# Four graph layers in one kernel: the two lookups of a slot placed side by side on TensorE

## The chip, the cores and the metric

The kernel runs on one core of a Trainium2 chip, in one launch. The metric is the device time of the launch in microseconds. The engines of the core are TensorE (PE, with its weight loads as PEld), VectorE (DVE), ScalarE (ACT), GpSimd (POOL) and SyncE (SP, which issues DMAs). [...]

## The reference

Sixteen graphs of 1024 nodes with 128 features pass through four layers; each adds its result to its input and normalizes the rows. Layer 0 is attention under an adjacency mask. Layer 2 is a sum over neighbours and a small network. Layer 3 first thins the adjacency row after row (each row's removals change later rows), then makes three convolutions. Layer 1 is the one that matters here:

```python
p = jnp.einsum('bnd,do->bno', x, W1 - W2)
q = jnp.einsum('bnd,do->bno', x, W2)
pre = p[:, :, None, :] + q[:, None, :, :] + b
h = jax.nn.relu(pre) * adj[..., None]
return jnp.max(h, axis=2)
```

For every node and feature it needs the maximum of `q` over the node's neighbours.

## The kernel before, in words

**The trick of layer 1.** The 1024 neighbours are cut into 86 groups of 12 (`NP`), each group into two of six. For six neighbours there are 64 subsets. For each of them a table holds the maximum of `q` over the subset (`tables_of`, lines 470 to 489, on DVE). Which subset a node has is found by a product of its adjacency with a matrix of plus and minus ones (`count`, line 814), turned into a one-hot row of 64 by ACT (line 815, tile `hot`). The lookup is then a product of table and one-hot (`look_up`, line 845) into a PSUM tile `pg`, and DVE keeps the running maximum in `best` (line 910; line 904 for a graph's first group).

**The slot.** One group of one graph is one slot; there are 16 x 86 = 1376 of them, written out by `slot(s, last)`. A slot has two halves, `h` 0 and 1, each for 512 of the 1024 nodes. The PE work of a half:

- a lookup of the half: four matmuls of 64 rows each, two with the table's high part and two with its low part, as the table is kept as two roundings; its `pg` is one of two buffers (tag "wide"), so it has to wait until DVE has read the lookup before the last;
- "pieces": a step or two of everything else (attention, the thinning of the adjacency, layer 2), handed out by `advance` and `dilate_on`;
- in odd slots, in half 0, `low_part(s + 1)` (line 834), which subtracts the rounded table from the exact one and needs ACT's `high` (line 829);
- the count of the same half two slots ahead (line 814), and behind it on ACT the `hot` of line 815;
- in even slots, in half 1, `table(s + 2)` (line 826), which transposes the table for two slots.

Counts and tables share two PSUM banks (tag "subset"). Their users take turns: in an even slot count 0, count 1, table; in the odd slot after it count 0, count 1. So the table takes the bank of the same slot's count 0, once ACT has made `hot` of it, and the second count of an odd slot takes the bank of the table before, once ACT has made `low` of it (line 836).

**What sets the order.** Around the slots stands a manual schedule for PE, ACT, DVE and POOL: their instructions keep the order in which the Python code issues them. Which pieces a half gets comes from a plan in units of slots: each stream asks with a cost and a delay, `room` limits what a half may take, and the thinning (`dilation`) asks to be continued at slot numbers (`due`). The plan knows no times, only slots. On SP and for DMAs the framework chooses the order.

**The thinning** runs beside the slots, 32 blocks of 32 rows. In each block POOL works through 31 rows one after the other (lines 669 to 679), starting when DVE has written `rest` (line 655). Its result goes out and in again by DMA (lines 686 and 689, tile `hit_p`), and DVE takes it up in line 703, at a place in its list that the plan fixed. POOL continues with line 707.

**After the slots** layer 3's convolutions follow (from line 942 on), which the change doesn't touch.

Of the kernel before, what the change touches and what calls it, by code (L numbers as in the profile page):

```python
# [29 lines left out]
F32 = mybir.dt.float32  # L30
# [10 lines left out]
P = 128  # L41
# [33 lines left out]
def tile_graph_layers(ctx: ExitStack, tc, a, out):  # L75
    nc = tc.nc
    x, adj, adjT = a["x"], a["adj"], a["adjT"]
    halves = (slice(0, 512), slice(512, 1024))
# [6 lines left out]
    psum = None  # L85
# [9 lines left out]
    psum = setup.enter_context(tc.tile_pool(name="psum0", bufs=2, space=PSUM))  # L95
# [146 lines left out]
    def layers_012():  # L242
# [3 lines left out]
        psum = psums.enter_context(tc.tile_pool(name="psumA", bufs=1, space=PSUM))  # L246
# [129 lines left out]
        def attend(b):  # L376
            for t in range(T):
                yield ask("PE", 0.01, after=("e", b, t))
                if t == 0:
                    y = w4.tile([P, T, D], F32, name="y0", tag="xT")  # L380
                e, total = exps.pop((b, t))
                eT = w4.tile([P, T, P], F32, name="eT")
                for h in range(2):
                    yield ask("PE", 0.44, take=True, same=(h == 0))
                    p = shared("pe")
                    for c in range(4):
                        nc.tensor.transpose(p[:, c * P:(c + 1) * P],  # L387
                                            e[:, (4 * h + c) * P:(4 * h + c + 1) * P], ident)
                    yield ask("A", 0.59, give=True, same=True)
                    nc.scalar.copy(eT[:, 4 * h:4 * h + 4, :].rearrange("p c i -> p (c i)"), p)  # L390
                happened["back", b, t] = now
                for h in range(4):
                    yield ask("PE", 0.45, take=(h == 0), same=(h > 0))
                    if h == 0:
                        pav = shared("pav")[:, :D]
                    for c in range(2 * h, 2 * h + 2):
                        nc.tensor.matmul(pav, eT[:, c, :], values[b][:, c, :], start=(c == 0), stop=(c == T - 1))  # L397
                yield ask("V", 0.4, give=True)
                share = small.tile([P, 1], F32, name="share")
                nc.vector.reciprocal(share, total)  # L400
                nc.vector.scalar_tensor_tensor(y[:, t, :], pav, share, X[b][:, t, :], op0=ALU.mult, op1=ALU.add)
            yield from norm(X[b], y)
            happened["X1", b] = now
# [66 lines left out]
        def tables_of(b):  # L470

            if b:
                yield ask("V", 0, urgent=True, after=("tables", b - 1))
            for g0 in range(0, NP, TG):
                n_g = 2 * min(TG, NP - g0)
                yield ask("V", 0.01, same=True, urgent=True, after=("q", b))
                made.append((b, g0))
                yield ask("V", 0.1, same=True, urgent=True, after=("used", *made[-3]) if len(made) > 2 else None)
                qg = qs[b].rearrange("o (g s) -> o g s", s=GS)
                subs[b, g0] = w2.tile([P, TG, P], F32, name="sub", bufs=2)  # L480
                sub = subs[b, g0].rearrange("o t (a s) -> o (t a) s", a=2)
                nc.vector.memset(sub[:, :n_g, 0:1], LOWEST)
                for k in range(GS):
                    n = 1 << k
                    yield ask("V", 0.06 + n * n_g / 960, same=(n < 8), urgent=True)
                    nc.vector.tensor_max(sub[:, :n_g, n:2 * n], sub[:, :n_g, 0:n],  # L486
                                         qg[:, 2 * g0:2 * g0 + n_g, k:k + 1].to_broadcast([P, n_g, n]))
                happened["sub", b, g0] = now
            happened["tables", b] = now
# [255 lines left out]
        def load_x(b):  # L745
            X[b] = apool.tile([P, T, D], F32, name="X", bufs=3)
            nc.sync.dma_start(out=X[b], in_=x[b].rearrange("(t p) d -> p t d", p=P))
# [5 lines left out]
        def load_columns(at):  # L753
            b, c = divmod(at, T + 1)
            if at > 1:
                before, k = divmod(at - 2, T + 1)
                rows = min(CH, N - k * CH)
                begin = len(nc.cur_bb.bb.instructions)
                nc.sync.dma_start(out=adj8[before][k * CH:k * CH + rows], in_=AT[at - 2][:rows])
                behind(nc.cur_bb.bb.instructions[begin - 1], begin)  # L760
            if b < B:
                rows = min(CH, N - c * CH)
                t = AT[at] = apool.tile([CH, N], F8, name="AT", bufs=4)
                if rows < CH:
                    nc.gpsimd.memset(t, 0.0)
                nc.gpsimd.dma_start(out=t[:rows], in_=adjT[b, c * CH:c * CH + rows])

        An, AT, subs, qs, ps, values, exps, bests, hots, tables = ({} for _ in range(10))
# [8 lines left out]
        def start(stream, first=False):  # L777
            pending[stream] = [next(stream, None), -9]
            streams.insert(0 if first else len(streams), stream)
# [59 lines left out]
        def look_up(s, h, pg):  # L839

            at = s % 2
            for k, part in enumerate(tables[s - at]):
                for a in range(2):
                    rows = slice(64 * a, 64 * a + 64)
                    nc.tensor.matmul(pg[:, a], part[rows, at * P:(at + 1) * P], hots[s][rows, halves[h]],  # L845
                                     start=(k == 0), stop=(k == 1))

        def merge(b, h):
            best, s = bests[b], halves[h]
            nc.vector.tensor_max(best[:, 0, s], best[:, 0, s], best[:, 1, s])  # L850
# [5 lines left out]
        def dilate_on():  # L856
            nonlocal due, wants_bank
            if due <= now and not (wants_bank and taken >= 2 and given.get(taken - 2, 1e9) > now):
                after, cost, wants_bank = next(dilate, (B * NP, 0, False))
                due += after  # L860
                room["V"] -= cost

        def slot(s, last):

            nonlocal now
            now = s
            b, g = divmod(s, NP)
            if s >= 0 and g == 0:
                bests[b] = bests[b - 1] if b else w4.tile([P, 2, N], F32, name="best")
                if b + 1 < B:  # L870
                    start(tables_of(b + 1), True)
                    load_x(b + 1)
                    start(attend(b + 1))
                    start(scores(b + 1))
            if s >= 0 and g % PC == 0:
                load_columns(b * (T + 1) + g // PC + 2)
            for h in range(2):
                now = s + 0.5 * h
                for e in ROOM:
                    room[e] = min(room[e] + ROOM[e] / 2, ROOM[e] / (2 if e in ("PE", "V") else 1))  # L880
                if s >= 0:
                    pg = psum.tile([P, 2, 512], F32, tag="wide", name="pg", bufs=2)
                    look_up(s, h, pg)
                early = s >= 0 and due < now
                if early:
                    dilate_on()
                advance(("PE",))
                advance(("A", "V", "Pool"))
                if s >= 0 and not early:
                    dilate_on()  # L890
                if h == 0 and s % 2 and s + 1 < last:
                    low_part(s + 1)
                if s + 2 < last:
                    count(s + 2, h)
                    if h and s % 2 == 0:
                        table(s + 2)
                if s >= 0:
                    own = bests[b][:, :, halves[h]]
                    if g == 0:
                        if b:  # L900
                            if h:
                                merge(b - 1, h)
                            total(b - 1, h)
                        nc.vector.tensor_copy(own, pg)
                        if b and h:
                            start(rest(b - 1))
                    else:
                        if g == NP - 1 and h:
                            merge(b, 0)
                        nc.vector.tensor_max(own, own, pg)  # L910
            if s >= 0:
                hots.pop(s)
# [19 lines left out]
        with tc.manual_schedule(engines={mybir.EngineType.PE, mybir.EngineType.Activation, mybir.EngineType.DVE,  # L932
# [43 lines left out]
            psum = ctx.enter_context(tc.tile_pool(name="psum", bufs=2, space=PSUM))  # L976
# [396 lines left out]
```

## Time and profile before

| what | value |
|---|---|
| time before, median of 3 runs | 6092.29 us (6090.22 to 6098.08) |
| time of the profiled execution | 6090.76 us |
| its span, first to last instruction | 6089.0 us |
| mean granted TensorE clock | 0.972 |
| busy over the span: PE, DVE, ACT, POOL | 5556.8, 4873.7, 3992.1, 3642.6 us |
| first lookup to last maximum | 139.8 to 4980.8 us, 4841 us |
| lookup matmuls (line 845), high and low | 5504 of 505 ns, 5504 of 400 ns |
| maxima (line 910) | 2720 of 1215 ns |

How to read it: a matmul's row gives the time from its issue to its modelled end, and matmuls overlap, so PE's cost of a step is read from start to start in the timeline and not from the durations. "PE" in a wait is the matmul, "PEld" the load of its weights. A wait "A <- B" is idle time of A's engine that ended when B was done; "issue" means that the profile shows no release. Waits that run beside other work are in the same list as waits that cost time.

### The profile page before, as it was taken

What the parts mean: (1) busy time and instruction counts of PE and PEld (TensorE: products, weight loads), DVE (VectorE), ACT (ScalarE), POOL (GpSimd) and SP (SyncE); (2) the same over time, 40 slices, a digit from 0 to 9 for tenths busy, and PEclk for the clock granted to TensorE, in tenths of its full rate; (3) what the DMA queues carried; (4) which work ended last, traced back from release to release, by engine and by line L of the source; (5) the groups of instructions that cost most, each with busy time, mean ns of one, the idle gap of its engine ahead of it and who ended that gap; (6) DMA issues with size and microseconds to landing.
All of it is one profiled execution on the core that took longest, in us unless ns stands there. A gap on an engine that the chain in (4) does not pass through costs nothing.

```text
span 6089.0 us, 93282 instructions
## 1 busy us (share of the span) xinstructions
PE 5556.8 (91%) x30144; PEld 3035.5 (50%) x30250; DVE 4873.7 (80%) x7484; ACT 3992.1 (66%) x7362; POOL 3642.6 (60%) x11879
## 2 busy tenths in 40 slices
PE   5989999999999999999999999999999878999998
PEld 4545454545454545454545454545444435555654
DVE  2888888889889888888888888888889865555455
ACT  3767777777677767677767676767666644444855
POOL 2676767677767767677777777777777641110114
PEclk8999999999999999999999999999999989999999
DMA  6121312121212121212121212121211025554645
GB/s 41 12 35 24 41 26 39 26 41 27 39 26 40 26 38 27 38 27 39 28 38 27 39 26 39 26 38 27 38 27 30 13 54 141 142 143 135 217 164 194
DMA packets 496976, 334.28 MB, mean 55 GB/s; under 512 B 303338, under 2 KB 448228, under 8 KB 492388
## 3 DMA queue, kind: packets, MB, share of 16 engines
q1 hardware_dynamic: 405504, 260.29, 14.6%
q0 software_dynamic: 89008, 67.42, 13.0%
q8 instruction: 237, 3.88, 0.3%
q14 instruction: 255, 2.09, 0.1%
q10 hardware_dynamic: 1972, 0.59, 0.1%
HBM read 362.38 MB, written 133.96 MB: 82 GB/s over the span
## 4 chain that ended last, share of the span: by engine, by line
PE 33%; DVE 11%; ACT 4%; issue 2%; POOL 1%; DMA 1%; SPq 0%; DVEq 0%; ACTq 0%; POOLq 0%
PE pg L845 8%; DVE best L910 5%; PE pagg L1073 5%; PE pm L814 3%; PE po L1103 2%; PE pa L439 1%; PE po L1097 1%; PE pav L397 1%; PE pp L300 1%; ACT hot L815 1%; DVE sub L486 1%; PE prank L599 1%; PE pdeg L1028 1%; DVE near L1016 1%; PE pe L387 1%
## 5 line engine op out<-in xcount | busy, mean ns | idle before, releaser
L910 DVE TENSOR_TENSOR best<-best,pg 128x1024 f32<-128x1024 f32 x2720 | 3260.8, 1215 | 481.2 <-PE pg L845 470.4
L815 ACT ACTIVATE hot<-pm,one_less 128x512 fp32r<-128x512 f32 x2752 | 1889.9, 690 | 728.7 <-PE pm L814 722.6
L845 PE MATMUL pg<-hot,high 64*128 64x512 f32 x5504 | 1400.3, 505 | 204.5 <-DVE best L910 174.6
L845 PE MATMUL pg<-hot,low 64*128 64x512 f32 x5504 | 1109.9, 400 | 0.0
L814 PE MATMUL pm<-AT,lit 120*128 120x512 fp8e4 x2752 | 1079.4, 392 | 4.5 <-ACT low L836 3.5
L845 PEld LDWEIGHTS pg<-hot,high 64*128 64x128 f32 x5504 | 521.2, 186 | 956.1 <-DVE best L910 455.6
L669 POOL TENSOR_SCALAR sc<-low_counts,half_mask,rest 16x1 f32<-16x1 f32 x992 | 361.0, 364 | 395.8 <-DVE rest L655 285.0
L845 PEld LDWEIGHTS pg<-hot,low 64*128 64x128 f32 x5504 | 534.5, 191 | 0.0
L814 PEld LDWEIGHTS <-lit 120*128 120x128 fp8e4 x2752 | 269.1, 98 | 385.5 <-issue 309.3
L674 POOL TENSOR_SCALAR sc<-sc 16x1 f32<-16x1 f32 x992 | 396.4, 400 | 104.9
L836 ACT CAST low<-pt 128x256 fp32r<-128x256 f32 x688 | 256.5, 373 | 254.0 <-PE pt L834 252.8
L671 POOL TENSOR_SCALAR sc<-sc 16x1 f32<-16x1 f32 x992 | 329.1, 332 | 107.4
L1118 POOL TENSOR_TENSOR length<-length,mhalf 128x8 f32<-128x8 f32 x48 | 78.9, 1645 | 486.2 <-DVE length L1117 486.2
L676 POOL TENSOR_SCALAR hit<-V,sc 16x31 bf16<-16x31 bf16 (+30 forms) x992 | 364.5, 367 | 0.0
L677 POOL TENSOR_SCALAR last_rank<-V,sc 16x31 f32<-16x31 bf16 (+30 forms) x992 | 346.9, 350 | 0.0
L834 PE MATMUL pt<-high,less 128*128 128x256 f32 x688 | 277.0, 403 | 67.4 <-ACT high L829 61.5
L486 DVE TENSOR_TENSOR sub<-sub,q 128x24 f32<-128x24 f32 (+11 forms) x768 | 306.8, 401 | 24.7 <-ACT q L304 10.5
L826 PE MATMUL pt<-ident,sub 128*128 128x128 f32 x1376 | 277.0, 283 | 53.2 <-ACT hot L815 51.1
L397 PE MATMUL pav<-v,eT 128*128 128x128 f32 x2048 | 301.5, 292 | 2.0 <-ACT eT L390 2.0
L397 PEld LDWEIGHTS pav<-v,eT 128*128 128x128 f32 x2048 | 255.5, 196 | 73.3 <-issue 55.6
L670 POOL TENSOR_SCALAR sc<-sc 16x1 f32<-16x1 f32 x992 | 239.9, 242 | 86.6
L349 PE MATMUL psc<-kT,qT 128*128 128x256 f32 x1024 | 273.9, 385 | 9.7 <-issue 9.7
(270 smaller groups left out, 9666.2 us busy)
## 6 DMA issues: line engine op xcount, KB each, us to landing
removed<-gone SPq DMA_DIRECT2D x128, 256.0 KB
An<-in_adj_dram POOLq DMA_DIRECT2D x16, 1024.0 KB, 15.0
E<-in_adj_dram POOLq DMA_DIRECT2D x128, 128.0 KB, 6.5
gone_all<-removed POOLq DMA_DIRECT2D x64, 256.0 KB, 10.5
near<-adj SPq DMA_DIRECT2D x16, 1024.0 KB
kept<-near SPq DMA_DIRECT2D x16, 1024.0 KB
share<-share SPq DMA_DIRECT2D x32, 512.0 KB
hidden<-r SPq DMA_DIRECT2D x32, 512.0 KB
```

The costliest lines, as they stand in the source:

```text
L397: nc.tensor.matmul(pav, eT[:, c, :], values[b][:, c, :], start=(c == 0), stop=(c == T - 1))
L486: nc.vector.tensor_max(sub[:, :n_g, n:2 * n], sub[:, :n_g, 0:n], qg[:, 2 * g0:2 * g0 + n_g, k:k + 1].to_broadcast([P, n_g, n]))
L669: gp.tensor_scalar(half, mine, half_mask[:, m], rest[:, n:n + 1], op0=ALU.mult, op1=ALU.add)
L671: gp.tensor_scalar(sf, half, 5.5, sf, op0=ALU.is_gt, op1=ALU.mult)
L674: gp.tensor_scalar(to, at, sf, none, op0=ALU.subtract, op1=ALU.subtract)
L676: gp.tensor_scalar(hit[:, n, n + 1:], V[:, n, n + 1:], at, None, op0=ALU.is_equal)
L677: gp.tensor_scalar(last[:, n + 1:], V[:, n, n + 1:], to, None, op0=ALU.is_le)
L814: nc.tensor.matmul(pm, lit[:, r, :], AT[b * (T + 1) + c][:, halves[h]], start=True, stop=True)
L815: nc.scalar.activation(hots[s][:, halves[h]], pm, AF.Relu, bias=one_less)
L845: nc.tensor.matmul(pg[:, a], part[rows, at * P:(at + 1) * P], hots[s][rows, halves[h]], start=(k == 0), stop=(k == 1))
L910: nc.vector.tensor_max(own, own, pg)
L1073: nc.tensor.matmul(pa[:, s], piece[:, t, :], m[c][:, s], start=(i == 0), stop=(i == 15))
```

## The change

Before, each half began with its own lookup. After, both lookups stand at the beginning of the slot, into the two `pg` buffers, and the pieces and the counts of both halves come behind them. DVE's maxima stay where they were, each at the end of its half. The whole diff:

```diff
@@ -878,9 +878,10 @@
                 now = s + 0.5 * h
                 for e in ROOM:
                     room[e] = min(room[e] + ROOM[e] / 2, ROOM[e] / (2 if e in ("PE", "V") else 1))
-                if s >= 0:
-                    pg = psum.tile([P, 2, 512], F32, tag="wide", name="pg", bufs=2)
-                    look_up(s, h, pg)
+                if s >= 0 and h == 0:
+                    pgs = [psum.tile([P, 2, 512], F32, tag="wide", name="pg", bufs=2) for _ in range(2)]
+                    for i in range(2):
+                        look_up(s, i, pgs[i])
                 early = s >= 0 and due < now
                 if early:
                     dilate_on()
@@ -895,7 +896,7 @@
                     if h and s % 2 == 0:
                         table(s + 2)
                 if s >= 0:
-                    own = bests[b][:, :, halves[h]]
+                    own, pg = bests[b][:, :, halves[h]], pgs[h]
                     if g == 0:
                         if b:
                             if h:
```

The number of instructions of PE, DVE, ACT and POOL is the same. The lists of DVE, ACT and POOL are the same in order too. On PE the second lookup of each slot moves ahead of the first half's pieces and count. On SP a few DMAs change places with their neighbours.

## The prediction

> **What bounds the kernel now.** I read the page's busy times first, then the groups of instructions, then the waits within the stretch of the slots (139.8 to 4980.8 us), then the timeline of PE and ACT in one slot.
>
> ```profile
> PE 5556.8 (91%) x30144; PEld 3035.5 (50%) x30250; DVE 4873.7 (80%) x7484; ACT 3992.1 (66%) x7362; POOL 3642.6 (60%) x11879
> ...
> L910 DVE TENSOR_TENSOR best<-best,pg 128x1024 f32<-128x1024 f32 x2720 | 3260.8, 1215 | 481.2 <-PE pg L845 470.4
> L815 ACT ACTIVATE hot<-pm,one_less 128x512 fp32r<-128x512 f32 x2752 | 1889.9, 690 | 728.7 <-PE pm L814 722.6
> L845 PE MATMUL pg<-hot,high 64*128 64x512 f32 x5504 | 1400.3, 505 | 204.5 <-DVE best L910 174.6
> ```
>
> PE and DVE wait for each other: DVE stood 470 us for lookups, PE 204.5 us for maxima. The slots take 4841 us for 1376, 3.518 us each. DVE is busy for 4259.4 us of that stretch (3.10 us a slot), and PE less its waits for DVE takes 3.518 - 204.5/1376 = 3.37 us. So PE is the longer lap, and it is not all work:
>
> ```profile
> DVE best L910 <- PE pg L845: 470.4, 839, 8.8
> PEld pg L845 <- DVE best L910: 455.6, 978, 12.1
> PEld pg L845 <- issue: 378.2, 1395, 1.0
> PEld L814 <- issue: 309.3, 819, 0.7
> POOL num L707 <- DVE counts L530: 289.6, 31, 21.6
> POOL sc L669 <- DVE rest L655: 285.0, 30, 15.5
> ```
>
> The two "issue" rows (total, times, longest) are weight loads that no semaphore held: those ahead of a lookup and those of a count. They stand where PE goes from 128 (or 120) rows to 64 and back. The timeline of an even slot without pieces on PE shows them as starts that lie 0.32 us apart:
>
> ```profile
> 2003.85 0.39 PE L814 MATMUL pm<-AT,lit 120*128 120x512 fp8e4 x1
> 2004.17 0.50 PE L845 MATMUL pg<-hot,high 64*128 64x512 f32 x2
> 2004.51 0.40 PE L845 MATMUL pg<-hot,low 64*128 64x512 f32 x2
> 2004.84 0.39 PE L814 MATMUL pm<-AT,lit 120*128 120x512 fp8e4 x1
> 2005.37 0.44 PE L826 MATMUL pt<-ident,sub 128*128 128x128 f32 x2
> ```
>
> and ACT in the same slot:
>
> ```profile
> 2003.88 0.87 ACT L282 ACTIVATE X<-y,ln_mv 128x128 f32<-128x128 f32 x2
> 2004.65 0.67 ACT L815 ACTIVATE hot<-pm,one_less 128x512 fp32r<-128x512 f32 x1
> ```
>
> Here the table (L826, 2005.37) starts 0.05 us after `hot` of the first count is done (2004.65 + 0.67): its bank came free just then. The reader is to see that the lookup at 2004.17 fills the time in which ACT makes that `hot`.
>
> [...] a count followed by a lookup lasts 0.32 us from start to start[...]. [...] The trace shows PE lookups waiting, 314 times, and nothing passing them.
>
> **The change, part by part.** Durations are those of the profiled execution, 6090.8 us with 1.8 us outside its span; the median is 1.5 us above it.
>
> *Switches (gain).* One of two visits to 64-row mode a slot goes. From start to start over all slots: lookup low to anything else 0.325, within a stream 0.216[...]; high to low 0.333 against 0.216, so 0.12 for the exposed first weights; a count before a lookup 0.32 against 0.216, 0.10; and the first load behind the second lookup is no longer exposed, 0.01 for fp8 or bf16 to 0.10 for f32, 0.035 in the mix. Sum 0.366 us a slot, x 1376 = 503 us of PE. All of it lies on PE's own lap.
>
> *Low part behind ACT (gain).* L834 waits for `high` (60.8 us of PE) and L826 for `hot` (51.1 us). I remove both rows, 112 us or 0.08 a slot; what L826 waits in the new order comes next.
>
> *The table behind the count (cost).* In an even slot the second lookup leaves the place between count 0 and the table. Read from each of the 688 even slots: from count 0 to the end of its `hot` 1.32 us in the median (1.12 to 1.76), ACT's queue included. PE has to fill that with two counts (0.43) and the second half's pieces, which 37% of these slots don't have. The mean wait is 0.65 us per even slot, 448 us. In the slot above it is 5.37 - 3.85 - 0.43 = 1.09. From below: take the room that the trace shows today between `hot` and table (some of it made by PE's waits for DVE) and shorten it by the 0.76 us that the lookup and its switches took: 317 us.
>
> *The second count behind low (cost).* In odd slots it takes the bank that ACT's `low` (L836) frees, 0.90 us after the low part's matmul. With the lookup gone, 0.43 us and the pieces lie between: 0.31 us per odd slot, 211 us; from today's room 160 us. Together 659 us (477 from below), 0.48 (0.35) a slot. PE's lap is then 3.37 - 0.37 - 0.08 + 0.48 = 3.40, or 3.27 with the lower waits: no gain, or a tenth of a microsecond. In slots with pieces PE gets faster, in bare ones slower.
>
> *The wait for DVE (cost).* The second lookup now starts 0.55 us after the first and needs the slot's last maximum before, which DVE reaches only at the end of that slot. From a second lookup that is not held: the first maximum starts 0.23 us later (a lookup's result reaches DVE 0.775 after its start), 1.135 for it (two of them take 2.35), the second half's other DVE work V (0 in a quarter of slots, 0.34 median, 1.0 at 90%), 1.20 and a 0.05 handover: 2.61 + V before the next second lookup can start. Slot by slot against PE's lap (2.3 to 4.5 us), PE is short of that in many slots: 0.20 us mean with the long lap, 0.27 with the short one. Behind the waiting lookup stand both halves' pieces, both counts and the table, and ACT and POOL behind those. Before, a lookup needed a maximum two lookups back with pieces between, and its fresh result was 2.0 us away against a lap of 3.3. So 3.60 or 3.54 a slot. Of today's 0.149 a slot of waits for DVE's backlog some remains: none to all; I take a tenth.
>
> *Moved past nothing.* DVE, ACT and POOL keep their order, so their queues cost nothing by themselves; the few SP transfers that change places have tens of microseconds of plan around them.
>
> *Sum.* (3.60 + 3.54)/2 + 0.015 = 3.585 us a slot, 0.067 more, x 1376 = +92 us: 6183 for the profiled execution, **6184 us** against the median. The bounds are 3.27 with no new DVE wait and 3.60 + 0.149.
>
> **The rivals.**
>
> *Faster: the ACT waits fall into DVE's.* If the waits for `hot` and `low` are paid in time that PE would stand for DVE anyway, DVE is the lap. Adding up, slot by slot, the longer of PE's work and DVE's work gives 3.51 for the kernel before (measured 3.518), which speaks for it; with 0.366 less PE work and no ACT waits it gives 3.37, -200 us. The thinning takes part back. POOL's 31 rows take 120.5 us a block, the DMA back about 4.5 more, and DVE comes for it 129.9 us after `rest`: only some 5 us of slack a block, and DVE already stood 10.5 us for it at 409 us. With slots 4% shorter 109 us are won there and 27 in the rest of the block: -136, **5956 us**. It decides if ACT is done within PE's own next 0.43 us plus pieces; L826's start on the heels of `hot` speaks against it. A half success (lower waits and half the DVE wait, 3.27 + 0.27/2 = 3.405, with the same cap about -100; with some backlog -50) lies near 6040.
>
> *No change.* Switches saved equal the waits gained and the DVE wait is one that exists today: **6092 us**.
>
> *Much slower.* All the backlog comes on top, as PE has no lead left: 3.60 + 0.149 = 3.75, +318, **6410 us**. Against it: the `hot`s are two slots ahead, and DVE is never without a lookup for longer than one handover when PE is the one that waits.
>
> That the change doesn't do what it says can be left out: the instruction list of the changed kernel has the two lookups side by side, each with its own wait for a maximum.
>
> **How the numbers follow.** Moderately slower 0.61 (own range 6105 to 6310), much slower 0.07, no change 0.08, faster 0.24 (0.11 of it below 6000). About 0.2% (12 us) is what can be told from no change here. So faster 0.24, same 0.08, slower 0.68; the range 6000 to 6310 leaves 0.11 below and 0.07 above.
>
> **What would show it.** The loads "issue" of L845 and L814 fall by half or more, high's mean stays near 505 for first lookups and drops to about 390 for second ones. L826's wait for `hot` rises from 51 to over 250 us, a wait of L814 for `low` appears (today 3.3 us), PE's wait for L910 grows above 175 us. POOL's waits for L655 and L707 grow with the slot. It is wrong if these ACT waits stay under 150 us, or if DVE's idle time for lookups falls below 300 us; then the switches were worth what they look like.

## The result, and the profile after

| | before | after |
|---|---|---|
| median of 4 runs | 6091.26 us (6088.10 to 6098.08) | 6195.36 us (6183.61 to 6205.61) |
| profiled execution, span | 6090.76, 6089.0 us | 6205.61, 6203.9 us |
| mean granted TensorE clock | 0.972 | 0.965 |
| first lookup to last maximum, per slot | 3.524 us | 3.606 us |
| everything else | 1240 us | 1243 us |

The stretch of the slots is counted here from the start of the first lookup (133.0 us in before) to the end of the last maximum, 4849 us before and 4961 after; the 4841 us given for before above run from the start of the first maximum (139.8) to that of the last.

After is slower: ratio 1.0169 (1.0148 to 1.0190), 104 us. Of the 115 us between the two profiled spans 112 lie in the slots. From the page of after, the lines that answer to those of before (the maxima's line is now L911):

```profile
PE 5426.3 (87%) x30132; PEld 3090.5 (50%) x30250; DVE 4853.2 (78%) x7484; ACT 3935.6 (63%) x7362; POOL 3619.0 (58%) x11879
...
L911 DVE TENSOR_TENSOR best<-best,pg 128x1024 f32<-128x1024 f32 x2720 | 3240.7, 1214 | 494.4 <-PE pg L845 485.3
L815 ACT ACTIVATE hot<-pm,one_less 128x512 fp32r<-128x512 f32 x2752 | 1856.6, 690 | 602.4 <-PE pm L814 591.5
L845 PE MATMUL pg<-hot,high 64*128 64x512 f32 x5504 | 1325.7, 477 | 254.8 <-DVE best L911 224.0
L814 PE MATMUL pm<-AT,lit 120*128 120x512 fp8e4 x2752 | 1043.0, 394 | 91.0 <-ACT low L836 84.5
...
L826 PE MATMUL pt<-ident,sub 128*128 128x128 f32 x1376 | 295.6, 297 | 219.3 <-ACT hot L815 213.3
```

The page of before has for the last two:

```profile
L814 PE MATMUL pm<-AT,lit 120*128 120x512 fp8e4 x2752 | 1079.4, 392 | 4.5 <-ACT low L836 3.5
...
L826 PE MATMUL pt<-ident,sub 128*128 128x128 f32 x1376 | 277.0, 283 | 53.2 <-ACT hot L815 51.1
```

PE is busy 130 us less and stands longer: within the slots it is without a matmul for 630 us, against 382 before. From the waits of after between 139.8 and 5095 us, the stretch of its slots (total, times, longest):

```profile
DVE best L911 <- PE pg L845: 485.3, 558, 5.0
...
POOL num L707 <- DVE counts L530: 369.4, 31, 25.6
...
PEld pg L845 <- issue: 235.7, 829, 3.3
PE pg L845 <- DVE best L911: 224.0, 396, 3.4
PE pt L826 <- ACT hot L815: 213.3, 355, 6.7
...
PEld L814 <- issue: 105.4, 279, 0.7
PE pm L814 <- ACT low L836: 84.3, 283, 1.4
```

Against before: the loads "issue" fell (378.2 to 235.7, 309.3 to 105.4), the table's wait for `hot` rose from 51.1 to 213.3, the count's wait for `low` from 3.3 to 84.3. The timeline shows how, on PE in an even slot of after and at the head of the next:

```profile
2041.96 0.40 PE L590 MATMUL pturn<-ident_b,E 128*128 128x128 bf16 x4
2042.19 0.60 PE L814 MATMUL pm<-AT,lit 120*128 120x512 fp8e4 x2
2043.68 0.44 PE L826 MATMUL pt<-ident,sub 128*128 128x128 f32 x2 [0.89 <-ACT hot L815]
2044.04 0.50 PE L845 MATMUL pg<-hot,high 64*128 64x512 f32 x2
2044.38 0.40 PE L845 MATMUL pg<-hot,low 64*128 64x512 f32 x2
2045.26 0.50 PE L845 MATMUL pg<-hot,high 64*128 64x512 f32 x2 [0.48 <-DVE best L911]
```

on ACT:

```profile
2042.45 0.59 ACT L591 CAST ET<-pturn 128x512 bf16<-128x512 f32 x1 [1.46 <-PE pturn L590]
2042.93 1.27 ACT L815 ACTIVATE hot<-pm,one_less 128x512 fp32r<-128x512 f32 x2
```

and on DVE:

```profile
2041.99 1.21 DVE L911 TENSOR_TENSOR best<-best,pg 128x1024 f32<-128x1024 f32 x1
2043.12 0.95 DVE L486 TENSOR_TENSOR sub<-sub,q 128x768 f32<-128x768 f32 x1
2043.99 1.21 DVE L911 TENSOR_TENSOR best<-best,pg 128x1024 f32<-128x1024 f32 x1
```

Two waits. The two counts now follow each other at once. So the table at 2043.68 starts as soon as the first `hot` is done, which ACT began only after `ET` and ended at 2042.93 + 0.69 = 2043.62. And the second lookup, due at about 2044.61, starts at 2045.26, 0.06 after the maximum that frees its buffer (2043.99 + 1.21 = 2045.20); the step `sub` of 0.95 us stands on DVE between the slot's two maxima.

**The accounting used below.** Bracketed idle times count from a matmul's modelled end. So I took, from the trace, the distances from start to start on PE between first lookup and last maximum. For each pair of neighbouring kinds the fast end (12th percentile) counts as work, the rest as a wait of the later matmul; at the half clock, which the trace records, up to as much again is put down to the clock (in after the matmuls of L349 start 0.215 us apart at full clock and 0.427 at half, in the median). In us of the slot stretch ("lookups" includes the longer distance from a lookup's `high` to its `low` behind a hold, over 0.33 us against 0.23):

| kernel | median, us | ratio to before (95%) | work | half clock | lookups | table | count | low part |
|---|---|---|---|---|---|---|---|---|
| before | 6091.26 | | 4146 | 87 | 245 | 74 | 23 | 92 |
| after | 6195.36 | 1.0169 (1.0148–1.0190) | 3745 | 125 | 411 | 319 | 171 | 18 |
| lookups parted by pieces | 6217.3 | 1.0188 (1.0173–1.0203) | 4061 | 93 | 237 | 292 | 119 | 14 |
| lookups mid-slot | 6252.11 | 1.0247 (1.0232–1.0262) | 4018 | 136 | 375 | 51 | 168 | – |
| maxima together | 6096.14 | 0.9994 (0.9983–1.0005) | 3761 | 91 | 284 | 325 | 180 | 29 |
| mid-slot, maxima together | 6129.65 | 1.0046 (1.0030–1.0061) | 4002 | 141 | 330 | 56 | 161 | – |
| counts first | 6394.88 | 1.0491 (1.0468–1.0514) | 3856 | 199 | 596 | 147 | 89 | 63 |
| counts first, maxima together | 6183.65 | 1.0145 (1.0125–1.0165) | 3853 | 164 | 364 | 141 | 101 | 94 |
| before, counts first | 6255.97 | 1.0261 (1.0240–1.0283) | 4230 | 143 | 255 | 4 | 4 | 214 |
| before, odd slots side by side | 6186.3 | 1.0146 (1.0125–1.0168) | 4049 | 157 | 367 | 84 | 78 | 9 |

The rows stand beside before's runs on the same chip, with medians of 6091.26 to 6100.05 us. After against before: work -401, clock +38, lookups +166, table +245, count +148, low part -74, the rest -10: +112, the difference of the two stretches (4961 - 4849).

The accounting has a blind spot: a wait that comes back with almost the same length in most cases of a pair is taken for work. The fast end of such a pair is then longer than that of the same pair in other kernels, and this shows three cases. In the two mid-slot kernels a count behind a table in 271 slots (0.825 us from start to start; in after a lookup follows a table after 0.200) hides some 169 us of waiting. With odd slots side by side, a count behind a count in 272 slots (0.616 against 0.220) hides 108 us. In the relieved kernels of before's order further down, a low part behind a lookup in 271 slots (0.54 and 0.55 against 0.32) hides 58 and 62 us.

### The profile page after: what moved, and what is told of

It reads as the page before. It is cut to its first block, busy times and chain, and to the rows that moved or that the text cites. A ratio compares the mean times of both kernels' runs of the same rounds, so it can differ in the third digit from the quotient of the medians.

```text
span 6203.9 us, 93371 instructions
## 1 busy us (share of the span) xinstructions
PE 5426.3 (87%) x30132; PEld 3090.5 (50%) x30250; DVE 4853.2 (78%) x7484; ACT 3935.6 (63%) x7362; POOL 3619.0 (58%) x11879
## 4 chain that ended last, share of the span: by engine, by line
PE 29%; DVE 12%; ACT 5%; issue 3%; POOL 2%; DMA 1%; SPq 0%; DVEq 0%; ACTq 0%; POOLq 0%
PE pg L845 6%; DVE best L911 6%; PE pagg L1074 5%; PE pm L814 2%; PE po L1104 2%; ACT hot L815 2%; PE pav L397 1%; PE po L1098 1%; PE pa L439 1%; DVE sub L486 1%; PE pt L826 1%; PE pdeg L1029 1%; DVE near L1017 1%; PE pp L300 1%; PE prank L599 1%
## 5 line engine op out<-in xcount | busy, mean ns | idle before, releaser
L911 DVE TENSOR_TENSOR best<-best,pg 128x1024 f32<-128x1024 f32 x2720 | 3240.7, 1214 | 494.4 <-PE pg L845 485.3
L815 ACT ACTIVATE hot<-pm,one_less 128x512 fp32r<-128x512 f32 x2752 | 1856.6, 690 | 602.4 <-PE pm L814 591.5
L845 PE MATMUL pg<-hot,high 64*128 64x512 f32 x5504 | 1325.7, 477 | 254.8 <-DVE best L911 224.0
L814 PE MATMUL pm<-AT,lit 120*128 120x512 fp8e4 x2752 | 1043.0, 394 | 91.0 <-ACT low L836 84.5
L845 PE MATMUL pg<-hot,low 64*128 64x512 f32 x5504 | 1119.3, 401 | 0.0
L845 PEld LDWEIGHTS pg<-hot,high 64*128 64x128 f32 x5504 | 530.0, 188 | 1094.1 <-DVE best L911 570.4
L669 POOL TENSOR_SCALAR sc<-low_counts,half_mask,rest 16x1 f32<-16x1 f32 x992 | 357.1, 360 | 400.9 <-DVE rest L655 299.6
L845 PEld LDWEIGHTS pg<-hot,low 64*128 64x128 f32 x5504 | 540.8, 191 | 30.4
L826 PE MATMUL pt<-ident,sub 128*128 128x128 f32 x1376 | 295.6, 297 | 219.3 <-ACT hot L815 213.3
L674 POOL TENSOR_SCALAR sc<-sc 16x1 f32<-16x1 f32 x992 | 394.7, 398 | 105.1
L826 PEld LDWEIGHTS pt<-ident,sub 128*128 128x128 f32 x1376 | 154.9, 143 | 487.9 <-ACT hot L815 465.3
L671 POOL TENSOR_SCALAR sc<-sc 16x1 f32<-16x1 f32 x992 | 318.5, 321 | 107.7
L814 PEld LDWEIGHTS <-lit 120*128 120x128 fp8e4 x2752 | 236.8, 100 | 189.6 <-issue 105.4
L834 PE MATMUL pt<-high,less 128*128 128x256 f32 x688 | 281.7, 409 | 13.3 <-ACT high L829 13.0
L670 POOL TENSOR_SCALAR sc<-sc 16x1 f32<-16x1 f32 x992 | 239.5, 241 | 86.5
```

The lines of the kernel that those rows point to most:

```text
L669: gp.tensor_scalar(half, mine, half_mask[:, m], rest[:, n:n + 1], op0=ALU.mult, op1=ALU.add)
L671: gp.tensor_scalar(sf, half, 5.5, sf, op0=ALU.is_gt, op1=ALU.mult)
L674: gp.tensor_scalar(to, at, sf, none, op0=ALU.subtract, op1=ALU.subtract)
L814: nc.tensor.matmul(pm, lit[:, r, :], AT[b * (T + 1) + c][:, halves[h]], start=True, stop=True)
L815: nc.scalar.activation(hots[s][:, halves[h]], pm, AF.Relu, bias=one_less)
L826: nc.tensor.matmul(pt[:, k * P:(k + 1) * P], subs[b, g0][:, g - g0 + k, :], ident, is_transpose=True, start=(k == 0), stop=(k == 1))
```

## The experiments

The theory: switches are really saved, and the saving is paid back to ACT (table and second count, whose bank comes free late) and to DVE (second lookup). The rivals: the saving is smaller than it looks, or one of the two payments is all of it.

**Lookups parted by pieces.** From after, the second lookup goes behind the first half's pieces: the switches are back, ACT's neighbours stay close.

```diff
                 if s >= 0 and h == 0:
                     pgs = [psum.tile([P, 2, 512], F32, tag="wide", name="pg", bufs=2) for _ in range(2)]
-                    for i in range(2):
-                        look_up(s, i, pgs[i])
+                    look_up(s, 0, pgs[0])
...
                     dilate_on()
+                if s >= 0 and h == 0:
+                    look_up(s, 1, pgs[1])
                 if h == 0 and s % 2 and s + 1 < last:
                     low_part(s + 1)
```

> The changed kernel with the second lookup put behind the first half's pieces and still ahead of its count. Where a half has pieces the second visit to 64-row mode is back, so little of the switch gain is left, and the second lookup has pieces between it and the first. The count and the table stay as close to each other as in the change, so PE has to wait for ACT. Theory (ACT waits of table and second count plus the wait for DVE): the ACT waits alone, some 0.38 us a slot, are paid with little gained: 6190 to 6330 us. Rival 1 (only the second lookup's wait for DVE costs): that wait is mostly gone, 5950 to 6110 us. Rival 2 (the saved switches are no time at all): as the change, about 6195 us.

Measured 6217.3 us, in the range of the theory; "as the change", rival 2's forecast, lies in that range too, so this time alone doesn't tell the two apart. Rival 1's forecast was missed. Work is up by 316 us against after, lookups wait as little as in before (237), and yet the kernel is as slow as after: table and count still wait 411 us, against before's 97. With only 85 us of work saved against before, the waits for ACT alone (table, count and low part 425 us against 189) are enough for a loss of 117 us.

**Lookups mid-slot.** From after, both lookups go between the first half's count and the second half's pieces, so that they fill the time of ACT's `hot`.

```diff
                 if s + 2 < last:
                     count(s + 2, h)
                     if h and s % 2 == 0:
                         table(s + 2)
+                if s >= 0 and h == 0:
+                    pgs = [psum.tile([P, 2, 512], F32, tag="wide", name="pg", bufs=2) for _ in range(2)]
+                    for i in range(2):
+                        look_up(s, i, pgs[i])
+                if h == 0 and s % 2 and s + 1 < last:
+                    low_part(s + 1)
```

(the same lines are taken out above.)

> The changed kernel with both lookups in the middle of the slot, between the first half's count and the second half's pieces (the low part behind them). Still one visit to 64-row mode, and the lookups fill the time between count 0 and the table. Theory: L826's wait for ACT goes (213 us of idle PE in the change), L814's wait for low stays near 84 us, part of the gain returns as waits for the maxima; 3.49 us a slot, 5990 to 6110 us. Rival 1 (only the wait for DVE costs): as the change, 6175 to 6215 us. Rival 2 (the saved switches are no time): not below the kernel before, 6090 us or more.

Measured 6252.11 us: the theory missed by over 140. The rows of its page for maxima, counts and tables:

```profile
L911 DVE TENSOR_TENSOR best<-best,pg 128x1024 f32<-128x1024 f32 x2720 | 3244.6, 1215 | 705.8 <-PE pg L845 699.1
...
L814 PE MATMUL pm<-AT,lit 120*128 120x512 fp8e4 x2752 | 1066.0, 393 | 245.0 <-ACT hot L815 205.5
...
L826 PE MATMUL pt<-ident,sub 128*128 128x128 f32 x1376 | 273.6, 280 | 38.2 <-ACT hot L815 37.7
```

The table's wait went (213.3 to 37.7), as expected; the count now waits 205.5 us for `hot`. In the new order an odd slot's first count comes right behind a table, and the bank it takes is that of the even slot's second count, just issued. In 271 slots without pieces this wait is so regular (0.625 us) that the accounting has it as work; with it the count waits some 340 us. Five tiles rotate through two banks, and the one gap that two lookups make is in front of one tile only. I moved the wait to another neighbour, and expected it to go.

**Maxima together.** From after, both maxima stand at the end of the first half on DVE; PE's order is after's.

```diff
-                if s >= 0:
-                    own, pg = bests[b][:, :, halves[h]], pgs[h]
+                for i in range(2 if s >= 0 and h == 0 else 0):
+                    own, pg = bests[b][:, :, halves[i]], pgs[i]
...
-                        if b and h:
-                            start(rest(b - 1))
...
+                if h and s >= NP and g == 0:
+                    start(rest(b - 1))
```

> The changed kernel with both maxima of a slot following each other on DVE at the end of the first half, so that the second half's other DVE work no longer lies between a lookup and the maximum that the next second lookup waits for. Only DVE's order differs. Theory: the second lookup's wait for DVE shrinks by up to 0.15 us a slot, PE's idle time for L911 falls from 224 to under 120 us, the ACT waits stay: 6000 to 6120 us. Rival 1 (the ACT waits alone cost, and the wait for DVE follows from them): within 25 us of the change, 6170 to 6220 us.

Measured 6096.14 us over 12 runs, ratio 0.9994 (0.9983 to 1.0005): the whole loss is gone. From its page:

```profile
L909 DVE TENSOR_TENSOR best<-best,pg 128x1024 f32<-128x1024 f32 x2720 | 3189.3, 1215 | 451.4 <-PE pg L845 445.0
...
L845 PE MATMUL pg<-hot,high 64*128 64x512 f32 x5504 | 1298.0, 468 | 167.0 <-DVE best L909 146.1
...
L826 PE MATMUL pt<-ident,sub 128*128 128x128 f32 x1376 | 296.9, 298 | 226.1 <-ACT hot L815 221.6
```

The wait for maxima falls from 224.0 to 146.1 (under 120 was expected); the table's 221.6 doesn't move. With the second maximum ahead of the second half's DVE pieces its buffer is free earlier. In the accounting lookups lose 127 us of waiting and the clock 34. What remains against before is work saved (-385) and waits for ACT gained (table, count, low part: 534 against 189): that leaves 40 us, which the lookups' 39 more take.

**Mid-slot with maxima together.** Both edits, the maxima at the end of the second half.

> Lookups in the middle of the slot, and both maxima at the end of its second half on DVE, behind the other work of both halves. Theory: both new waits are mostly gone and the one saved visit to 64-row mode remains; DVE's work (3.1 us a slot) and POOL's chain of rows set the end: 5880 to 5990 us, and DVE waits for hit_p (L703) in more than ten of the 32 blocks. Rival 2 (the saved switches are no time): 6060 to 6110 us. Rival 1 as in the run with the maxima together: near 6050 us.

Measured 6129.65 us, above the range: the count's wait is as in the mid-slot kernel (161, and the same 169 us hidden in the work). DVE waited for `hit_p` in 2 blocks, where over ten were expected. The order on DVE is worth 122 us here.

**Counts first.** From after, the low part and the counts go ahead of the pieces, which are then to fill the time of `hot`; an odd slot's second count stays behind them.

```diff
+                if h == 0:
+                    if s % 2 and s + 1 < last:
+                        low_part(s + 1)
+                if s + 2 < last and not (h and s % 2):
+                    count(s + 2, h)
                 early = s >= 0 and due < now
...
-                if h == 0 and s % 2 and s + 1 < last:
-                    low_part(s + 1)
-                if s + 2 < last:
-                    count(s + 2, h)
-                    if h and s % 2 == 0:
+                if s + 2 < last and h:
+                    if s % 2:
+                        count(s + 2, h)
+                    else:
                         table(s + 2)
```

> The changed kernel with the counts and the low part put ahead of the half's pieces (only the second count of an odd slot stays behind its pieces), so that pieces lie between count 0 and the table and between the low part and the count that takes its bank. DVE's order is that of the change. Theory (ACT waits and the wait for DVE both cost): PE's idle time for hot at L826 and for low at L814, 298 us together in the change, falls under 90 us; a part comes back as waits for maxima; 5990 to 6080 us. Rival 1 (only the second lookup's wait for DVE costs, ACT waits lie beside it): 6175 to 6215 us as the change.

Measured 6394.88 us, the slowest of these kernels and over 300 us above the range. Its waits over the whole span:

```profile
ACT hot L815 <- PE pm L814: 846.3, 940, 4.0
...
PE pg L845 <- DVE best L915: 362.1, 509, 9.6
...
PE pe L387 <- ACT e L359: 95.6, 58, 2.7
PE pt L826 <- ACT hot L815: 91.4, 188, 0.6
```

The table's wait fell from 213.3 to 91.4, which was the point (with `low`'s 33.8 it is 125, where under 90 was expected). What made it slower I read like this, without a run that shows it: ACT's `hot` now stands in its list ahead of its pieces. When a held second lookup holds the count behind it, ACT stands at `hot` (846.3 us against 591.5 in after), its pieces start late, PE waits for those (95.6 against 29.1 in after), and DVE's steps behind them are late too, and with them the next maximum (362.1 against 224.0). That ACT stands at `hot` is no loss by itself: in before it did so for 722.6 us. I had looked at PE's order alone.

**Counts first with maxima together**, the edit of above on this kernel.

> As the run with the counts ahead of the pieces, and both maxima of a slot together at the end of its first half on DVE. Theory: both new waits are reduced, the saved switches stay: PE's lap near 3.1 us, DVE's work and POOL's chain near 3.1 to 3.4 us: 5900 to 5990 us. Rival 1: as the run with the maxima together alone, 6080 to 6110 us. Rival 2 (the saved switches are no time): not under the run that has the lookups apart and the counts ahead.

Measured 6183.65 us: 211 us better than without, but far above the range.

**Before, with counts first**: the same move in the kernel before.

> The kernel before with nothing changed but the counts and the low part put ahead of the half's pieces: lookups apart, two visits to 64-row mode a slot. It has only the 112 us of ACT waits of the kernel before to lose. Theory: 6030 to 6090 us, and the run with lookups together, counts ahead and maxima together is at least 60 us faster than this one, as it saves 0.366 us of switches a slot. Rival 2 (the saved switches are no time): the two within 30 us of each other, or this one faster.

Measured 6255.97 us, 160 us slower than before, so counts first is bad by itself: work +84, low part +122 (PE's wait of L834 for ACT's `high` is 177.4 us, against 60.8 in before), clock +56, against 89 less for table and count. The side-by-side kernel with the same counts and with its maxima together is faster than this one by 72 us (over 60 was expected), but without the moved maxima it is slower by 139. So the gain is that of both moves together, and what the maxima's order is worth with the lookups apart wasn't run.

**Banks.** In the whole kernel the lookups hold four PSUM banks (a bank here is a buffer of 128x512 f32), counts and tables two, everything else two; I ran no version of it with more for counts and tables. The four kernels below make room: as their expectation says, they leave out one of the two groups of a lookup with its maximum, and 15 of POOL's 31 row steps in each block. In before's trace the matmuls of the two groups start 0.003 us apart, so PE's distances were to stay without the second; its work by the accounting did (4212 to 4216 us in before's order against 4146, 3749 to 3752 in after's against 3745). DVE (busy 53 to 57% of the span) and POOL (34 to 37%) are then far from limiting. Two have before's order, two after's; one of each has four banks. The lines of the edit that matter here, four banks first:

```diff
-            pm = psum.tile([P, 512], F32, tag="subset", name="pm", bufs=2)
+            pm = psum.tile([P, 512], F32, tag="subset", name="pm", bufs=4)
...
-            pt = psum.tile([P, 512], F32, tag="subset", name="pt", bufs=2)[:, :2 * P]
+            pt = psum.tile([P, 512], F32, tag="subset", name="pt", bufs=4)[:, :2 * P]
...
-                for a in range(2):
+                for a in range(1):
                     rows = slice(64 * a, 64 * a + 64)
```

> The kernel before with DVE and POOL relieved, so that PE and ACT set the slot: it leaves out the second group of six in each lookup and maximum [...], and all but 16 of the 31 row steps of each block on POOL; the PSUM tile of a lookup is then one bank. Two banks for counts and tables, as before. Theory: PE's lap of before without waits for DVE, 3.2 to 3.37 us a slot: 5640 to 5880 us.

> The changed kernel with the same work left out (second group of six in lookups and maxima, 15 of the 31 row steps on POOL), two banks for counts and tables. Theory: PE's lap of the change is no shorter, as the switches saved are paid back in waits for hot and low: within 2% of the relieved kernel before, 5640 to 5920 us. Rival 1 (the ACT waits lie beside the wait for DVE and cost nothing by themselves): 0.37 us a slot less than the relieved kernel before, some 500 us.

> The relieved kernel before (same work left out) with four PSUM banks for counts and tables in place of two, from the banks that the smaller lookup leaves free. Theory: only the 112 us of waits for hot and high of before are touched: 0 to 120 us below the relieved kernel before with two banks.

> The relieved changed kernel (same work left out) with four PSUM banks for counts and tables. No table or count waits for the bank of its neighbour now. Theory: waits of L826 for hot and L814 for low under 20 us, and the saved switches come out: 350 to 520 us below the relieved changed kernel with two banks and below the relieved kernel before with four banks. Rival 1: as the relieved changed kernel with two banks. Rival 2 (saved switches are no time): not below the relieved kernel before with four banks.

| relieved kernel | median, us | granted clock | work | half clock | lookups | table + count |
|---|---|---|---|---|---|---|
| before's order, 2 banks | 6716.9 | 0.840 | 4216 | 827 | 125 | 57 |
| after's order, 2 banks | 6332.07 | 0.882 | 3749 | 535 | 197 | 435 |
| before's order, 4 banks | 6587.05 | 0.852 | 4212 | 739 | 122 | under 25 |
| after's order, 4 banks | 6084.48 | 0.893 | 3752 | 464 | 346 | under 25 |

(The first three medians are of 2 runs each, and those of the first lie 87 us apart.) Levels and most differences missed, because the clock fell: the first one, with work left out, is slower than the whole kernel, at a granted clock of 0.840 against 0.972 (more on this in the last section). With two banks after's order was to be within 2% of before's and is 385 us faster, which is nearer to rival 1's 500 us. But of the 339 us between their profiled executions the half clock takes 292, so this pair doesn't decide between theory and rival. What the four do tell: after's order has 460 to 467 us less work on PE, 398 to 409 when the low part's hidden wait is taken out, as in the whole kernel (401). And with two banks it has 378 us more waits of tables and counts. Counts and tables of after's order with two banks, then with four, from their pages (lines one further down here):

```profile
L815 PE MATMUL pm<-AT,lit 120*128 120x512 fp8e4 x2752 | 1142.6, 432 | 72.8 <-ACT low L837 66.5
...
L827 PE MATMUL pt<-ident,sub 128*128 128x128 f32 x1376 | 324.7, 322 | 185.6 <-ACT hot L816 182.0
```

```profile
L815 PE MATMUL pm<-AT,lit 120*128 120x512 fp8e4 x2752 | 1082.2, 428 | 0.0
...
L827 PE MATMUL pt<-ident,sub 128*128 128x128 f32 x1376 | 293.6, 298 | 0.0
```

Idle times of 66.5 and 182.0 go to zero with the banks, and 248 us of wall time with them (in before's order 130, of which the clock's part of the accounting is 88); 350 at least was expected. Of the more than 410 us that table and count no longer wait, 149 come back as waits of lookups (197 to 346). With four banks after's order is 503 us faster than before's, which was expected of it; how much of that is the clock (464 against 739) can't be taken out cleanly. So the waits of table and count are a matter of banks: more banks take them away, and time with them.

**Odd slots side by side.** From before: in odd slots lookups and maxima are together, in even ones apart, so that the table keeps its lookup in front.

```diff
+                mine = range(2) if s % 2 and h == 0 else () if s % 2 else (h,)
...
+                for i in mine if s >= 0 else ():
+                    pgs.append(psum.tile([P, 2, 512], F32, tag="wide", name="pg", bufs=2))
+                    look_up(s, i, pgs[i])
```

> The kernel before, with the two lookups put together (and the two maxima together on DVE at the end of the first half) in odd slots only; even slots, which make the table, keep the second lookup between count 0 and the table. Theory: the table's wait for hot stays as in the kernel before (51 us of idle PE), about half of the 400 us of PE work is saved and the low part's wait for high goes, the second count's wait for low comes (85 us of idle PE): 5960 to 6060 us, below both kernels. Rival 1 (the wait for DVE is what counts; with the maxima together it is gone, and the ACT waits cost nothing): no faster than the run that has maxima together and lookups together in all slots, 6080 us or more.

Measured 6186.3 us, a miss. The table waits 84 us as hoped. The work saved is 97 us by the accounting and 205 with the 108 hidden ones, so the expected half of 400 did come, and the second count waits some 186 us for `low`, near after's 171 (85.0 of it on the page, as expected). What I had left out is that the second lookup of an odd slot is held by 303 us, in half as many slots as in after (398): ahead of it stands the second lookup of the even slot, whose maximum comes only at that slot's end. All lookups together wait 122 us more than in before, and the half clock takes 70 more. Rival 1's number (6080 or more) came, but not its reason, as the wait for DVE was not gone. No version of the whole kernel that I ran is faster than before by more than can be measured.

## Why the prediction was right

It said 6184 us and slower, by switches that are real and two payments that outweigh them; measured 6195.36. The mechanism held, but that the number is within 11 us is partly luck. In the slots 92 us more were forecast and 112 measured. The forecast (middle of its two versions) was 503 saved by switches, 456 paid to ACT net of the old waits and 139 to DVE; measured are 401, 319 and 166, and 28 for clock and rest. So 102 us too much saving stood against 137 too much paid to ACT. The terms:

- *Switches*, -503: measured -401. The longer distance from start to start behind a lookup (0.325 us against 0.216) gave 131 of 151, that from `high` to `low` (0.333 against 0.216) 145 of 165, that from a count to a lookup (0.32 against 0.216) 125 of 138; the fourth term, 48 us at the first load behind the second lookup, did not show. I had counted every slot; a second lookup that is held has the longer distance from `high` to `low` again (0.332 us or more in the slowest quarter, 0.233 in the median), which the accounting has under lookups.
- *Low part behind ACT*, old waits of L834 and L826, -112: L834 fell from 92 to 18 in the accounting, so this holds but for a rest. The old waits were larger than the page's idle times (92 and 74 in the accounting against 60.8 and 51.1).
- *Table behind the count*, 448 or 317 from below: measured 319. *Second count behind low*, 211 or 160: measured 171. The version that shortened the room seen in the trace of before was right, the one worked from medians too high by a third. One of its readings was off: from count 0 to the end of its `hot` the trace of before has 1.17 us in the median (1.11 to 1.74 from 10% to 90%), not 1.32. The relieved kernels show the cause: with four banks these waits are gone.
- *Wait for DVE*, 0.20 to 0.27 us a slot (275 to 371 us) and a tenth of the backlog (21): measured 398 for second lookups, 65 of it the longer distance from `high` to `low` behind the hold, and 13 for first ones. Against it I had taken off the 204.5 us that PE stood ahead of lookups in before (the line puts 174.6 of it down to maxima); the accounting has 245. That the hold comes from DVE is shown by moving the maxima: 99 us less than after, 108 when each is set against before's runs beside it.
- *Not in the sum*: the clock. 319 us of the stretch ran at half clock against 236, worth 38 us of PE.

*The rivals.* "Faster" stood or fell with ACT being done within PE's next 0.43 us plus pieces; the whole kernel shows 490 us of waits against that, and the kernel with four banks what happens if it holds. "Half success" needed half the DVE wait and the lower ACT waits: the maxima-together kernel is close to it, and gets 6096 where I had put some 6040. "Much slower" needed all the backlog on top; first lookups wait 13 us.

*Of the signs named.* "Issue" loads of L814 fell by two thirds, those of L845 by 38%, less than half; high's mean is 506 ns for first lookups, 448 for second ones (394 in the median: the held ones lift the mean); the table's idle time of 213.3 stayed below the 250 I named, as that figure counts from the modelled end; PE's wait for maxima rose above 175 (224.0); POOL's waits grew (289.6 to 369.4, 285.0 to 299.6). Neither sign against it came: the ACT waits are 298 us, DVE's idle time 485.

*What stays open.* Clock and waits come together, so the 38 us are an attribution and not an experiment. A third bank for counts and tables in the whole kernel wasn't tried, so the banks' part is shown in the relieved kernels alone. Nor was before run with its maxima moved together.

## What to carry to other kernels

Placing TensorE's 64-row matmuls side by side saved four fifths of what the start-to-start distances said here (401 of 503 us), but with two banks for counts and tables the saving was paid back: they waited 490 us, and under 25 with four banks in the relieved kernels. So where tiles that lose the work between them take turns in the same PSUM banks, count for every tile what stands between it and the release of its bank by the engine that reads it. A group also wants its consumers grouped: a second lookup placed at the front needs its maximum moved to the front as well, or it waits for all that DVE does in between (99 to 211 us here). Moving one tile along the list, without more banks, mostly handed the wait to the next one here (mid-slot, idle PE at the table went from 213.3 to 37.7 us, and the count waited 205.5 us for `hot`).

## What the runs showed of the hardware

I had not expected that a kernel with work left out can run slower on PE. The traces record the granted clock of TensorE, and PE's idle time can be set beside its stretches at half clock. Within the slots, from first lookup to last maximum:

| | before | after |
|---|---|---|
| stretches at half clock | 30 | 58 |
| their time | 236 us | 319 us |
| PE without a matmul, share of the whole | 8% | 13% |
| the same in the 5 us ahead of a stretch at half clock, mean | 41% | 39% |

So in both kernels the falls to half clock came behind a few microseconds with much idle PE, and after, which has more idle time, has more of them. That fits with waits that cost more than their own length here, by some 38 us of clock in the accounting.

Idle time by the accounting's waits is not all of it. The relieved kernel in before's order waits less than before does (lookups 125 us, table and count 57, against 245 and 97), and its granted clock is 0.840 against 0.972, with 827 us put down to half clock against 87. Which part of the work left out brought that about was not shown by a run.
